# The last 64 features of the fp4 down product: split factors in rounded float32

## The chip, the cores and the metric

The kernel runs on one core of a Trainium2 chip. The metric is the device time of one execution in microseconds (us); the time before is the median of three runs, 2608.18 us (2606.8 to 2610.64). The engines are named TensorE (PE in the profile; its weight loads PEld), VectorE (DVE), ScalarE (ACT), GpSimd (POOL) and SyncE (SP, which issues most DMAs; SPq is its queue).

## The reference

The reference is a stack of six residual blocks on x of 8 x 1024 tokens with 256 features. The change concerns the first and the third block, which are the same feed-forward with fp4 quantization:

```python
def fp4_quant_dequant(x):              # blocks of 16 along the last dim
    scale = max(max(abs(xb)) / 6.0, 1e-12)
    idx = searchsorted(_MID, abs(xb / scale))
    return _GRID[idx] * sign(xb) * scale
...
gate = fp4_linear(x, w_gate)           # 256 -> 704
y = fp4_linear(x, w_up)                # 256 -> 704
h = silu(gate) * y
return fp4_linear(h, w_down)           # 704 -> 256, both sides quantized
...
x = x + 0.5 * _L0_ffn_ref(_layernorm(x), ...)
```

Between them lies a linear attention with decay, behind them a ternary feed-forward, an attention with memories, and the ternary feed-forward again.

## The kernel before

All of x stays on the chip as 16 groups X[g] of 4 tiles of 128 tokens, 64 tiles in all. `ffn_fp4` runs twice, once as the first stage (`prepare` true, when it also prepares weights for itself and later stages) and once as the third. It is one loop of steps: step i makes the hidden features of tile i and works off earlier tiles.

In step i TensorE makes the gate product pg and the up product pu for two halves of 352 features (L835, float32). ScalarE applies silu (L846), VectorE multiplies into h (L848). VectorE takes the blocks' maxima and their reciprocals (L783 to L787), and GpSimd divides h by its scales (L791). In step i+1 ScalarE writes the magnitudes into a PSUM area qp (L795) and VectorE rounds in two operations, the second into a bfloat16 grid gd (L858). gd has 768 columns for 704 features: the last 64 are filled with zeros once.

The grid is turned by DMA, not by TensorE. TensorE transposes only the scales (pts, L863), ScalarE copies them to sct (L869), and SP issues, in this order: sct to DRAM (sd, L871), the grid's DMA transpose gt (L884), and a load that spreads each scale over its 16 features (ht, L876, 384 KB). Two steps later GpSimd multiplies ht by gt (`scaled_turn`, L899). One step after that `down` makes the product po of six chunks of 128 features by wd (L932), and VectorE adds it to X (L941). The last chunk holds 64 features; its other rows are zeros in ht and in wd. The last two tiles take another way (`turn`): TensorE transposes h itself.

The normalized inputs go the same way, in halves of a group. Every odd step ScalarE normalizes two tiles (L317, L325, four operations) for a group two ahead; GpSimd divides them by their scales in the even step; in the next odd step ScalarE and VectorE round them to a grid gx in the same memory (mgx, L795 and L858). SP turns it in the even step after that (gtx, L1048), behind gt and ht. The next normalizing of that half overwrites the grid and so waits for gtx, and so does GpSimd's product xt (L899).

The order on each engine is written out by hand: `pin` ties every instruction to the one before it on its engine, so an engine that waits holds back everything behind it. `copies` is a list of ScalarE copies that are issued after the first silu of the next step. Weights for the down product are rounded and turned in steps 1 to 5 of the first stage (`prep_down_scale`, `prep_down`, `prep_down_turn`).

Of the kernel before, what the change touches and what calls it, by code (L numbers as in the profile page):

```python
# [9 lines left out]
F32 = mybir.dt.float32  # L10
F32R = mybir.dt.float32r
# [3 lines left out]
ALU = mybir.AluOpType  # L15
# [3 lines left out]
P = 128  # L19
D = 256  # L20
# [3 lines left out]
G = 4  # L24
# [15 lines left out]
def macaron_kernel(  # L40
# [25 lines left out]
    nc = tc.nc  # L66
    NB, S, _ = x.shape
# [3 lines left out]
    NI = w_gate.shape[0]  # L71
# [5 lines left out]
    DCH = [(k, min(P, NI - k)) for k in range(0, NI, P)]  # L77
    NC = len(DCH)
# [17 lines left out]
    w_f0 = f0_stack.enter_context(tc.tile_pool(name="w_f0", bufs=1))  # L96
# [43 lines left out]
    wd_n = raw.tile([P, 2, NI], F32, name="wd_n")  # L140
# [32 lines left out]
    ident = const.tile([P, P], F32, name="ident")  # L173
# [57 lines left out]
    pin, behind = order_keeper()  # L231
# [209 lines left out]
    def turned_part(xt, k):  # L441
        return xt.rearrange("p (j k) t -> p k j t", k=2)[:, k]

    wd = w_f0.tile([P, NC, D], F32, name="wd")
    nc.gpsimd.memset(wd[DCH[-1][1] :, NC - 1, :], 0.0)
    with (
        tc.tile_pool(name="prep_ps", bufs=2, space=PSUM, side="right") as prep_ps,
        tc.tile_pool(name="prep_pq", bufs=1, space=PSUM, side="right") as prep_pq,
# [160 lines left out]
        for k in range(2):  # L609
            pt = prep_ps.tile([P, TG], F32, tag="pt", name="pt")  # L610
# [22 lines left out]
    def prep_down(c):  # L633
        fp4_round(wd_n[:, c, :], wd_sc.pop(c), raw, nc.gpsimd, pin)

    def prep_down_turn(ps, tag):
        for i, (k0, kn) in enumerate(DCH):
            pt = ps.tile([P, D], F32, tag=tag, name="ptd")
            for c in range(2):
                pin(  # L640
                    nc.tensor.transpose(
                        pt[:kn, c * P : (c + 1) * P], wd_n[:, c, k0 : k0 + kn], ident
                    )
                )
            pin(nc.scalar.copy(wd[:kn, i, :], pt[:kn, :]))


    def load_a0():
# [96 lines left out]
    def ffn_fp4(prepare, after):  # L745
        with ExitStack() as st:
# [8 lines left out]
            xts, hs, hts = {}, {}, {}  # L755
# [1 line left out]


            gd = gp.tile([P, NC * P], BF16, name="gd")
            nc.gpsimd.memset(gd[:, NI:], 0.0)  # L760
            scales = []
            for n in range(2):
                sc = gp.tile([P, P], F32, name=f"sc_{n}")
# [12 lines left out]
            DOWN = 5  # L776
            HT_BUFS = DOWN if prepare else 4

            def scale(v, pool, at, mul=nc.gpsimd, sc=None):
                vb = v.rearrange("p (b k) -> p b k", k=16)  # L780
                _, nb, _ = vb.shape
                am, sp = qp[:, at : at + nb], qp[:, at + nb : at + 2 * nb]
                pin(nc.vector.tensor_reduce(am, vb, AX.X, ALU.max, apply_absolute_value=True))  # L783
                pin(nc.vector.tensor_scalar(sp, am, -1.0 / 6.0, -1e-12, ALU.mult, ALU.min))
                rs = pool.tile([P, nb], F32, tag="q_rs", name="q_rs")
                pin(nc.vector.tensor_scalar(rs, sp, -FP4_TIE, None, ALU.mult))
                pin(nc.vector.reciprocal(rs, rs))  # L787
                if sc is None:
                    sc = pool.tile([P, nb], F32, tag="q_sc", name="q_sc")
                copies.append(lambda: pin(nc.scalar.copy(sc, sp)))  # L790
                pin(mul.tensor_tensor(vb, vb, rs[:, :, None].to_broadcast([P, nb, 16]), ALU.mult))  # L791
                return sc

# [72 lines left out]
            def spread(i, pt):  # L866

                sct = hp.tile([P, P], F32, tag="sct", name="sct", bufs=1)
                pin(nc.scalar.copy(sct, pt))  # L869
                sd = dp.tile([8, 16, P], F32, tag="sd", name="sd")  # L870
                pin(nc.sync.dma_start(out=sd.rearrange("b c t -> c b t"), in_=sct))  # L871

                def wide(out, c0, c1):
                    part = sd[:, c0:c1, :].rearrange("b c t -> b (c t)")
                    pin(
                        nc.sync.dma_start(  # L876
                            out=out.rearrange("p c t -> p (c t)"),
                            in_=part[:, None, :].to_broadcast([8, 16, (c1 - c0) * P]),
                        )
                    )  # L880

                def turn_grid():
                    gt = hp.tile([P, NC, P], BF16, tag="gt", name="gt", bufs=2)
                    pin(nc.sync.dma_start_transpose(out=gt, in_=gd))  # L884
                    turning[i] = gt

                turn_grid()
                ht = hp.tile([P, NC, P], F32, tag="ht", name="ht", bufs=HT_BUFS)
                wide(ht, 0, NC)
                spreading[i] = ht  # L890
                if i in xhalf:
                    to, half = xhalf.pop(i)
                    if half == 0:
                        xts[to] = lnp.tile([P, 2 * G, P], F32, tag="xt", name="xt")
                    wide(xts[to][:, G * half : G * half + G, :], NC, NC + G)

            def multiplied(wide, grid):
# [4 lines left out]
                    )  # L902
                )

            def scaled_turn(i):
                hs.pop(i)
                ht = spreading.pop(i)
                multiplied(ht, turning.pop(i))
                hts[i] = (ht, P)

            def turn(i):
                h, _ = hs.pop(i)
                ht = hp.tile([P, NC, P], F32, tag="ht", name="ht", bufs=HT_BUFS)
                for c0, c1 in ((0, 4), (4, 5), (5, 6)):
                    kn = DCH[c0][1]
                    pa = ps_t.tile([P, 4, P], F32, tag="pt", name="pt")
                    for c in range(c0, c1):
                        k0 = DCH[c][0]
                        pin(
                            nc.tensor.transpose(pa[:kn, c - c0, :], h[:, k0 : k0 + kn], ident)  # L920
                        )
                    pin(nc.scalar.copy(ht[:kn, c0:c1, :], pa[:kn, : c1 - c0, :]))
                hts[i] = (ht, DCH[-1][1])

            def down(i, ps=ps_o, tag="po"):
                g, j = divmod(i, G)
                ht, tail = hts.pop(i)
                po = ps.tile([P, D], F32, tag=tag, name="po")
                for c in range(NC):
                    kn = tail if c == NC - 1 else P  # L930
                    pin(
                        nc.tensor.matmul(  # L932
                            po,
                            lhsT=ht[:kn, c, :],
                            rhs=wd[:kn, c, :],
                            start=(c == 0),
                            stop=(c == NC - 1),
                        )
                    )
                pin(  # L940
                    nc.vector.scalar_tensor_tensor(  # L941
                        X[g][:, j, :], po, 0.5, X[g][:, j, :], ALU.mult, ALU.add
                    )
                )
# [49 lines left out]
            for i in range(NT + 3):  # L994
# [82 lines left out]
                if i < NT:  # L1077
                    own = scales[i % 2] if by_dma(i) else None
                    if own is not None:
                        scale(h, hp, NI, sc=own[:, : NI // 16])  # L1080
                        hs[i] = (h, own)
                    else:
                        hs[i] = (h, scale(h, hp, NI) if i < NT - 1 else None)

                    if j % 2 == 0 and i > 1:
                        to_s, half_s = ((i + 6) // G, 0) if j == 2 else ((i + 4) // G, 1)
                        if 1 < to_s < NG:
                            scale(
                                x_part(half_s), lnp, NI + 88,
                                sc=own[:, NC * 8 : NC * 8 + 2 * D // 16],  # L1090
                            )
                            xhalf[i] = (to_s, half_s)
                    if j % 2 == 1 and i > 1:
                        to_r, half_r = ((i + 5) // G, 0) if j == 3 else ((i + 3) // G, 1)
                        if 1 < to_r < NG:
                            v = x_part(half_r)
                            mg = ps_t.tile([P, 2 * D], F32, tag="pt", name="mgx")
                            magnitudes(v, mg)
                            gx = v.bitcast(BF16)[:, 0 : 2 * D]
                            round_grid(v, mg, gx)  # L1100
                            xgrids[to_r, half_r] = (gx, i)
                    if i == 0:
                        nb = 2 * D // 16
                        for n in range(2):
                            round_(
                                v1[:, 2 * D * n : 2 * D * (n + 1)],
                                sc1[:, nb * n : nb * (n + 1)], mgs[n],
                            )
                    ln.advance(i, 0)
                    if NT - 18 <= i < NT - 2:  # L1110
                        begin(after, NT - 2 - i)
                if prepare and i == DOWN:
                    prep_down_turn(ps_t, "pt")
                if i >= DOWN or not prepare:
                    first = downs
                    while downs <= (i - 4 if i < NT else i - 3) and downs < first + 2:
# [968 lines left out]
```

## Time and profile before

| what | value |
|---|---|
| median of three runs | 2608.18 us |
| the profiled execution | 2604.35 us |
| its span, first to last instruction | 2602.6 us |
| PE busy | 2504.2 us, 96% |
| DVE busy | 2107.9 us, 81% |
| ACT busy | 1235.8 us, 47% |
| POOL busy | 902.6 us, 35% |
| mean granted TensorE clock | 0.994 |

The span is what lies between the first and the last instruction on the slowest core; what the execution takes beyond it (1.75 us) lies outside. Busy shares are averages over six stages with different limits, so a stage's own windows tell more. A group of instructions is shown as line, engine, operation, output<-inputs, shapes, count, then total busy time and the mean of one in ns, then the idle time of the engine ahead of it and what ended it. A float32 matmul appears as two rows. The mean of one matmul includes its way through the array; how fast they follow one another is read from the chain or the timeline. In the timeline a row begins with its start and its length, both in us.

### The profile page before, as it was taken

How to read it: one execution, taken by the hardware profiler on the slowest of the kernel's cores; microseconds unless marked ns; L12 is line 12 of the kernel's file. 1: busy time of each engine (PE TensorE's matmuls, PEld its weight loads, DVE VectorE, ACT ScalarE, POOL GpSimd, SP SyncE). 2: the span in 40 equal slices, each digit the busy share in tenths (PEclk: the TensorE clock that was granted, in tenths of full speed). 3: DMA queues.
4: the chain of work that ended last, by engine and by line, in shares of the span. 5: the costliest groups of instructions: out<-in, count | busy, mean ns of one | idle time of the engine just before them, and what ended most of it. 6: DMA issues, size and time to landing. Idle time of an engine off the chain costs nothing.

```text
span 2602.6 us, 52695 instructions
## 1 busy us (share of the span) xinstructions
PE 2504.2 (96%) x20426; PEld 1864.2 (72%) x20426; DVE 2107.9 (81%) x5040; ACT 1235.8 (47%) x2785; POOL 902.6 (35%) x895
## 2 busy tenths in 40 slices
PE   4899999999999998999999999999999999999999
PEld 2566776766666665677777789995677767678998
DVE  7899999858777678998889789657888888879864
ACT  5344444433433333444444366665555555437664
POOL 4555555521100102555555400004555555540000
PEclk9899999999999999999999999999999999999999
DMA  7455565510000001556555300000000000000001
GB/s 218 99 111 120 119 114 112 110 32 2 2 2 2 2 2 29 113 117 116 115 114 118 81 1 1 1 1 1 2 2 2 2 2 2 2 2 25 33 33 42
DMA packets 197883, 130.32 MB, mean 50 GB/s; under 512 B 137824, under 2 KB 173696, under 8 KB 197632
## 3 DMA queue, kind: packets, MB, share of 16 engines
q1 hardware_dynamic: 196688, 125.75, 22.3%
q8 instruction: 161, 2.64, 0.4%
q0 software_dynamic: 240, 0.54, 0.1%
q14 instruction: 90, 0.74, 0.1%
q10 hardware_dynamic: 704, 0.66, 0.1%
HBM read 78.67 MB, written 16.52 MB: 37 GB/s over the span
## 4 chain that ended last, share of the span: by engine, by line
PE 80%; DVE 11%; ACT 3%; DMA 3%; issue 2%; POOL 1%; SPq 1%; DVEq 0%; POOLq 0%; ACTq 0%
PE po L932 10%; PE po L1207 9%; PE pg L835 9%; PE ph L1180 9%; PE pu L835 8%; PE sc L1250 5%; PE py L1334 5%; PE pq L1348 4%; PE pkv L1348 4%; PE pk L1348 4%; PE po L1348 4%; PE py L1316 2%; PE pmo L1765 2%; DVE at L1259 1%; DMA gtx<-xn 1%
## 5 line engine op out<-in xcount | busy, mean ns | idle before, releaser
L835 PE MATMUL pg<-wgu,xt 128*128 128x352 f32 x1024 | 350.0, 465 | 13.4 <-ACT sg L846 13.1
L932 PE MATMUL po<-wd,ht 128*128 128x256 f32 x1536 | 356.0, 382 | 2.3 <-DVE x L941 1.8
L835 PE MATMUL pu<-wgu,xt 128*128 128x352 f32 x1024 | 348.9, 464 | 2.1 <-DVE h L848 1.9
L932 PEld LDWEIGHTS po<-wd,ht 128*128 128x128 f32 x1536 | 291.7, 191 | 66.0 <-issue 4.1
L791 POOL TENSOR_TENSOR h<-h,q_rs 128x704 f32<-128x704 f32 (+1 forms) x128 | 176.3, 1378 | 419.9 <-DVE q_rs L787 419.9
L846 ACT ACTIVATE sg<-pg 128x352 f32<-128x352 f32 x256 | 117.8, 460 | 399.3 <-PE pg L835 394.0
L835 PEld LDWEIGHTS pg<-wgu,xt 128*128 128x128 f32 x1024 | 194.9, 192 | 108.5 <-ACT sg L846 21.1
L835 PEld LDWEIGHTS pu<-wgu,xt 128*128 128x128 f32 x1024 | 187.1, 193 | 103.3 <-issue 14.7
L1207 PE MATMUL po<-w,hl 128*128 128x256 f32 x1024 | 243.9, 280 | 1.4 <-DVE hl L1191 1.2
L1207 PE MATMUL po<-w,hh 128*128 128x256 f32 x1024 | 243.4, 280 | 0.0
L1881 POOL TENSOR_TENSOR mo<-mo 128x256 f32<-128x256 f32 x192 | 164.3, 856 | 195.0 <-DVE mo L1778 186.5
L899 POOL TENSOR_TENSOR ht<-gt,ht 128x768 f32<-128x768 bf16 x124 | 206.4, 1664 | 0.0
L1180 PE MATMUL ph<-xh,w 128*128 128x512 f32 x512 | 204.4, 401 | 1.4 <-ACT hf L1188 0.6
L1180 PE MATMUL ph<-xl,w 128*128 128x512 f32 x512 | 202.2, 396 | 0.0
L1191 DVE TENSOR_TENSOR hl<-hf,hh 128x512 fp32r<-128x512 f32 x256 | 168.2, 683 | 39.6 <-ACT hh L1189 36.1
L1207 PEld LDWEIGHTS po<-w,hl 128*128 128x128 f32 x1024 | 192.1, 188 | 4.5 <-DVE hl L1191 2.5
L1207 PEld LDWEIGHTS po<-w,hh 128*128 128x128 f32 x1024 | 192.0, 188 | 2.6 <-DVE x L1215 0.3
L848 DVE TENSOR_TENSOR h<-sg,pu 128x352 f32<-128x352 f32 x256 | 131.6, 514 | 60.0 <-PE pu L835 53.1
L1188 ACT ACTIVATE hf<-ph,b1c 128x512 f32<-128x512 f32 x256 | 168.3, 696 | 18.5 <-PE ph L1180 16.1
L1259 DVE TENSOR_TENSOR at<-sc,dec 128x512 f32<-128x512 f32 x256 | 158.5, 681 | 16.6 <-PE sc L1250 16.5
L1259 DVE TENSOR_TENSOR at<-sc,tri 128x512 f32<-128x512 f32 x256 | 164.6, 678 | 0.4 <-PE sc L1250 0.4
L1189 ACT CAST hh<-hf 128x512 fp32r<-128x512 f32 x256 | 149.2, 628 | 17.0 <-PE po L1207 15.2
(276 smaller groups left out, 5304.0 us busy)
## 6 DMA issues: line engine op xcount, KB each, us to landing
ht<-sd SPq DMA_DIRECT2D x124, 384.0 KB
xt<-sd SPq DMA_DIRECT2D x56, 256.0 KB
sd<-sct SPq DMA_DIRECT2D x124, 64.0 KB
x<-in_x SPq DMA_DIRECT2D x15, 512.0 KB
out<-x SPq DMA_DIRECT2D x15, 512.0 KB
raw_w<-in_w_t SPq DMA_DIRECT2D x2, 1024.0 KB
gt<-gd SPq DMA_TRANSPOSE x124
gtx<-xn SPq DMA_TRANSPOSE x56
```

The source lines that it names most:

```text
L791: pin(mul.tensor_tensor(vb, vb, rs[:, :, None].to_broadcast([P, nb, 16]), ALU.mult))
L835: nc.tensor.matmul(ps, lhsT=xts[g][:, 2 * j + k, :], rhs=wgu[:, k, (2 * q + of_up) * NHALF : (2 * q + of_up + 1) * NHALF], start=(k == 0), ...
L899: nc.gpsimd.tensor_tensor(wide.rearrange("p c t -> p (c t)"), grid.rearrange("p c t -> p (c t)"), wide.rearrange("p c t -> p (c t)"), ALU. ...
L932: nc.tensor.matmul(po, lhsT=ht[:kn, c, :], rhs=wd[:kn, c, :], start=(c == 0), stop=(c == NC - 1),)
L1180: nc.tensor.matmul(ph, lhsT=w1[:, k, f * P : (f + 1) * P], rhs=xt[:, k, :], start=(k == 0 and xt is xh), stop=(k == 1 and xt is xl),)
L1188: nc.scalar.activation(hf, ph, AF.Gelu, bias=b1c[:, f : f + 1])
L1189: nc.scalar.copy(hh[:, f, :], hf)
L1191: nc.vector.tensor_tensor(hl[:, f, :], hf, hh[:, f, :].bitcast(F32), ALU.subtract)
L1207: nc.tensor.matmul(po, lhsT=ht[:, f, j * P : (j + 1) * P], rhs=w2[:, f, :], start=(f == 0 and ht is hh), stop=(f == NF - 1 and ht is hl),)
L1259: nc.vector.tensor_tensor(at, sc.rearrange("p m (e t) -> p (m e) t", e=2), weight, ALU.mult)
L1348: nc.tensor.matmul(dst, lhsT=lhsT, rhs=rhs, start=n == 0, stop=n == len(parts) - 1)
L1881: summed = nc.gpsimd.tensor_tensor(mo[:, :, :, 0, :], mo[:, :, :, 0, :], mo[:, :, :, m, :], ALU.add)
```

## The change

The last 64 features of the down product fill the whole array. Their rows stand twice in both factors: in gd the last 64 columns are copied behind themselves, and so are the last four scales, so ht's last chunk holds the 64 features twice. The weight tile ws holds, for the same 64 features, the rounded high part (float32r) in its first 64 rows and the remainder in its last 64. ht's last chunk is split for every tile into hh, its rounding to float32r (ScalarE), and hl, the remainder (GpSimd). The last float32 matmul of `down` becomes two float32r matmuls, hh by ws and hl by ws, whose sum is (high + remainder) x (high + remainder).

The fills with zeros go. `prep_down_turn` makes ws through a spare tile; `turn` doubles the last 64 features on GpSimd before its transposes, and moves its transposes into two groups of three.

```diff
-    wd = w_f0.tile([P, NC, D], F32, name="wd")
-    nc.gpsimd.memset(wd[DCH[-1][1] :, NC - 1, :], 0.0)
+    NK = DCH[-1][1]
+    wd = w_f0.tile([P, NC - 1, D], F32, name="wd")
+    ws = w_f0.tile([P, D], F32R, name="ws")
...
-    def prep_down_turn(ps, tag):
+    def prep_down_turn(ps, tag, pool):
+        spare = pool.tile([P, G, D], F32, tag="xn1", name="wt", bufs=1)
+        wt = spare[:, 0, :].rearrange("p (c n k) -> p c n k", c=2, n=2)
+        for c in range(2):
+            pin(nc.gpsimd.tensor_copy(
+                    wt[:, c], wd_n[:, c, None, NI - NK :].to_broadcast([P, 2, NK])))
...
+                wh = spare[:, 1, :].bitcast(F32R)
+                pin(nc.scalar.copy(wh, pt))
+                pin(nc.scalar.copy(ws[:NK], pt[:NK]))
+                pin(nc.vector.tensor_tensor(
+                        ws[NK:], pt[NK:], wh[NK:].bitcast(F32), ALU.subtract))
...
-            nc.gpsimd.memset(gd[:, NI:], 0.0)
...
-                copies.append(lambda: pin(nc.scalar.copy(sc, sp)))
+                copies.append(lambda: pin(nc.scalar.copy(sc[:, :nb], sp)))
+                if tail:
+                    copies.append(
+                        lambda: pin(nc.scalar.copy(sc[:, nb : nb + tail], sp[:, nb - tail :])))
...
+                pin(nc.scalar.copy(gd[:, NI:], gd[:, NI - NK : NI]))
                 turn_grid()
...
+            def split(ht):
+                hh = hp.tile([P, P], F32R, tag="hh", name="hh", bufs=3 if prepare else 2)
+                pin(nc.scalar.copy(hh, ht[:, NC - 1, :]))
+                hl = hp.tile([P, P], F32R, tag="hl", name="hl", bufs=3 if prepare else 2)
+                pin(nc.gpsimd.tensor_tensor(
+                        hl, ht[:, NC - 1, :], hh.bitcast(F32), ALU.subtract))
+                return hh, hl
+
             def scaled_turn(i):
                 hs.pop(i)
                 ht = spreading.pop(i)
                 multiplied(ht, turning.pop(i))
-                hts[i] = (ht, P)
+                hts[i] = (ht, *split(ht))
...
             def turn(i):
...
+                hd = lnp.tile([P, G, D], F32, tag="xn1", name="hd", bufs=1)[:, 0, 0:P]
+                pin(nc.gpsimd.tensor_copy(hd[:, 0:NK], h[:, NI - NK :]))
+                pin(nc.gpsimd.tensor_copy(hd[:, NK:], h[:, NI - NK :]))
-                for c0, c1 in ((0, 4), (4, 5), (5, 6)):
+                for c0, c1 in ((0, 3), (3, NC)):
...
             def down(i, ps=ps_o, tag="po"):
...
-                for c in range(NC):
-                    kn = tail if c == NC - 1 else P
+                factors = [(ht[:, c, :], wd[:, c, :]) for c in range(NC - 1)]
+                factors += [(hh, ws), (hl, ws)]
+                for n, (left, right) in enumerate(factors):
...
-                        scale(h, hp, NI, sc=own[:, : NI // 16])
+                        scale(h, hp, NI, sc=own, tail=NK // 16)
```

More of the change, by code (lines that the diff above doesn't have):

```diff
@@ L634, in prep_down @@
         fp4_round(wd_n[:, c, :], wd_sc.pop(c), raw, nc.gpsimd, pin)
-    def prep_down_turn(ps, tag):
-        for i, (k0, kn) in enumerate(DCH):
+    def prep_down_turn(ps, tag, pool):
+        spare = pool.tile([P, G, D], F32, tag="xn1", name="wt", bufs=1)
+        wt = spare[:, 0, :].rearrange("p (c n k) -> p c n k", c=2, n=2)
+        for c in range(2):
+            pin(
+                nc.gpsimd.tensor_copy(
+                    wt[:, c], wd_n[:, c, None, NI - NK :].to_broadcast([P, 2, NK])
+                )
+            )
+        for i, (k0, _) in enumerate(DCH):
             pt = ps.tile([P, D], F32, tag=tag, name="ptd")
             for c in range(2):
-                pin(
-                    nc.tensor.transpose(
-                        pt[:kn, c * P : (c + 1) * P], wd_n[:, c, k0 : k0 + kn], ident
+                if i < NC - 1:
+                    part = wd_n[:, c, k0 : k0 + P]
+                else:
+                    part = wt[:, c].rearrange("p n k -> p (n k)")
+                pin(nc.tensor.transpose(pt[:, c * P : (c + 1) * P], part, ident))
+            if i < NC - 1:
+                pin(nc.scalar.copy(wd[:, i, :], pt))
+            else:
+                wh = spare[:, 1, :].bitcast(F32R)
+                pin(nc.scalar.copy(wh, pt))
+                pin(nc.scalar.copy(ws[:NK], pt[:NK]))
+                pin(
+                    nc.vector.tensor_tensor(
+                        ws[NK:], pt[NK:], wh[NK:].bitcast(F32), ALU.subtract
                     )
                 )
-            pin(nc.scalar.copy(wd[:kn, i, :], pt[:kn, :]))
     def load_a0():
@@ L777, in ffn_fp4, with scale @@
             HT_BUFS = DOWN if prepare else 4
-            def scale(v, pool, at, mul=nc.gpsimd, sc=None):
+            def scale(v, pool, at, mul=nc.gpsimd, sc=None, tail=0):
                 vb = v.rearrange("p (b k) -> p b k", k=16)
@@ L789, in scale @@
                     sc = pool.tile([P, nb], F32, tag="q_sc", name="q_sc")
-                copies.append(lambda: pin(nc.scalar.copy(sc, sp)))
+                copies.append(lambda: pin(nc.scalar.copy(sc[:, :nb], sp)))
+                if tail:
+                    copies.append(
+                        lambda: pin(nc.scalar.copy(sc[:, nb : nb + tail], sp[:, nb - tail :]))
+                    )
                 pin(mul.tensor_tensor(vb, vb, rs[:, :, None].to_broadcast([P, nb, 16]), ALU.mult))
@@ L903, in multiplied @@
                 )
+            def split(ht):
+                hh = hp.tile([P, P], F32R, tag="hh", name="hh", bufs=3 if prepare else 2)
+                pin(nc.scalar.copy(hh, ht[:, NC - 1, :]))
+                hl = hp.tile([P, P], F32R, tag="hl", name="hl", bufs=3 if prepare else 2)
+                pin(
+                    nc.gpsimd.tensor_tensor(
+                        hl, ht[:, NC - 1, :], hh.bitcast(F32), ALU.subtract
+                    )
+                )
+                return hh, hl
             def scaled_turn(i):
@@ L913, in turn @@
                 ht = hp.tile([P, NC, P], F32, tag="ht", name="ht", bufs=HT_BUFS)
-                for c0, c1 in ((0, 4), (4, 5), (5, 6)):
-                    kn = DCH[c0][1]
-                    pa = ps_t.tile([P, 4, P], F32, tag="pt", name="pt")
-                    for c in range(c0, c1):
[L918 to L923, printed above, removed]
+                hd = lnp.tile([P, G, D], F32, tag="xn1", name="hd", bufs=1)[:, 0, 0:P]
+                pin(nc.gpsimd.tensor_copy(hd[:, 0:NK], h[:, NI - NK :]))
+                pin(nc.gpsimd.tensor_copy(hd[:, NK:], h[:, NI - NK :]))
+                for c0, c1 in ((0, 3), (3, NC)):
+                    pa = ps_t.tile([P, 3, P], F32, tag="pt", name="pt")
+                    for c in range(c0, c1):
+                        part = h[:, c * P : (c + 1) * P] if c < NC - 1 else hd
+                        pin(nc.tensor.transpose(pa[:, c - c0, :], part, ident))
+                    pin(nc.scalar.copy(ht[:, c0:c1, :], pa[:, : c1 - c0, :]))
+                hts[i] = (ht, *split(ht))
             def down(i, ps=ps_o, tag="po"):
                 g, j = divmod(i, G)
-                ht, tail = hts.pop(i)
+                ht, hh, hl = hts.pop(i)
                 po = ps.tile([P, D], F32, tag=tag, name="po")
-                for c in range(NC):
-                    kn = tail if c == NC - 1 else P
+                factors = [(ht[:, c, :], wd[:, c, :]) for c in range(NC - 1)]
+                factors += [(hh, ws), (hl, ws)]
+                for n, (left, right) in enumerate(factors):
                     pin(
                         nc.tensor.matmul(
[L933 to L937, printed above, removed]
+                            po, lhsT=left, rhs=right, start=(n == 0), stop=(n == NC)
                         )
@@ L1112, in ffn_fp4 @@
                 if prepare and i == DOWN:
-                    prep_down_turn(ps_t, "pt")
+                    prep_down_turn(ps_t, "pt", lnp)
                 if i >= DOWN or not prepare:
```

## The prediction

> **What bounds the kernel now.** First the page: its span, the chain of work that ended last, and the group that the edit rewrites.
>
> ```profile
> span 2602.6 us, 52695 instructions
> ...
> PE 80%; DVE 11%; ACT 3%; DMA 3%; issue 2%; POOL 1%; SPq 1%; DVEq 0%; POOLq 0%; ACTq 0%
> ...
> L932 PE MATMUL po<-wd,ht 128*128 128x256 f32 x1536 | 356.0, 382 | 2.3 <-DVE x L941 1.8
> ```
>
> TensorE is 80% of the chain. The down product has 1536 rows for 2 stages x 64 tiles x 6 chunks = 768 float32 matmuls, so each is two passes. I then asked for busy time in the second fp4 stage's steady part.
>
> ```profile
> 1104.80:1476.70 371.90, 371.90 (x1451) 268.95 (x1451) 324.90 (x720) 155.78 (x392) 202.39 (x147) 1.00 0.56 114
> ```
>
> TensorE (second number) is busy in all 371.90 us at full granted clock, VectorE in 324.90 (87%), ScalarE 155.78, GpSimd 202.39. So a step (one 128-token tile) is as long as TensorE's work in it. The chain in order of time prices a pass; its columns are start, length, work.
>
> ```profile
> 1104.78 2.59 PE po L932 x12
> ...
> 1535.32 3.77 PE po L1207 x32
> ```
>
> Twelve float32 passes take 2.59 us (0.216 each); 32 passes of rounded float32 (float32r), same shape, take 3.77 (0.118 each). Last, the timeline of two steps (start, length, engine, line, work, then idle time before it and its releaser), from which every link below is read.
>
> ```profile
> 1312.98 2.75 PE L932 MATMUL po<-wd,ht 128*128 128x256 f32 x12
> ...
> 1313.21 1.24 SPq L884 DMA_TRANSPOSE gt<-gd  x1
> ...
> 1314.59 0.60 SPq L876 DMA_DIRECT2D ht<-sd  x1
> ...
> 1315.24 1.20 SPq L1048 DMA_TRANSPOSE gtx<-xn  x1
> ...
> 1317.69 0.76 ACT L795 ACTIVATE qp<-h 128x704 f32<-128x704 f32 x1
> ...
> 1318.21 1.66 POOL L899 TENSOR_TENSOR ht<-gt,ht 128x768 f32<-128x768 bf16 x1
> ...
> 1319.57 0.89 DVE L858 SCALAR_TENSOR_TENSOR gd<-qp,h 128x704 bf16<-128x704 f32 x1
> ...
> 1319.69 0.26 ACT L869 COPY sct<-pts 128x128 f32<-128x128 f32 x1
> ...
> 1320.18 0.51 ACT L317 ACTIVATE xn<-x,ln_b 128x256 f32<-128x256 f32 x1 [0.23 <-DMA gtx<-xn]
> ...
> 1320.32 1.16 POOL L899 TENSOR_TENSOR xt<-gtx,xt 128x512 f32<-128x512 bf16 x1 [0.44 <-DMA gtx<-xn]
> ...
> 1320.42 2.75 PE L932 MATMUL po<-wd,ht 128*128 128x256 f32 x12
> ...
> 1322.08 0.58 ACT L795 ACTIVATE mgx<-xn 128x512 f32<-128x512 f32 x1
> ...
> 1323.23 1.39 POOL L791 TENSOR_TENSOR h<-h,q_rs 128x704 f32<-128x704 f32 x1 [1.75 <-DVE q_rs L787]
> ...
> 1324.39 0.46 ACT L846 ACTIVATE sg<-pg 128x352 f32<-128x352 f32 x1 [1.74 <-PE pg L835]
> ...
> 1325.04 0.76 ACT L795 ACTIVATE qp<-h 128x704 f32<-128x704 f32 x1
> ...
> 1326.09 0.88 DVE L858 SCALAR_TENSOR_TENSOR h<-qp,h 128x704 f32<-128x704 f32 x1
> ...
> 1327.00 0.89 DVE L858 SCALAR_TENSOR_TENSOR gd<-qp,h 128x704 bf16<-128x704 f32 x1
> ...
> 1328.09 1.24 SPq L884 DMA_TRANSPOSE gt<-gd  x1
> ```
>
> Step length: product to product, 1320.42 - 1312.98 = 7.44 us, two steps 14.87. Steps alternate. An odd one (the one of 1320) normalizes two tiles on ScalarE (1320.18 to 1322.08), and that waits for the turned x grid (gtx) that SP issued in the even step before; GpSimd multiplies xt with the same grid. In the present order GpSimd is free of ScalarE here: xt starts 0.14 us after the normalizing starts.
>
> **What it removes.** Per tile one float32 chunk, 2 x 0.216 = 0.432 us, becomes two float32r passes, 2 x 0.118 = 0.236: 0.196 us less, 25.1 us for 128 tiles. If float32r cost as much here as float32 passes the gain would be 0; if streaming alone counts, as in the hidden product's 32 passes of twice the width (7.47 us in the same chain, so 0.117 per 256 columns), it is the same 0.196. I take 0.196: a step could fall to 7.24, two to 14.48. Three fills with zeros go as well, ahead of everything that waits: 0.
>
> **What it adds to a step.** ScalarE: a 64-column copy inside gd (nearest row: L790, 44 columns, 0.19; I take 0.20), behind VectorE's gd and ahead of the grid's transpose on SP; a 4-column copy (at most that 0.19), off the path while the next ScalarE work waits for GpSimd; and hh, 128x128 (nearest row sct, 128x128, 0.26; bounds 0.19 and 0.35). GpSimd: hl, 128x128. By its two-input rows of 256 columns (731 ns, L1968) and 1024 (2374 ns, L1470), 2.14 ns a column, 0.46 us; bounds 0.40 and the nearest in width, 0.65 (L1659, 128 columns, another operation). TensorE uses hl in the next step, some 4 us later: no wait there. DMA sizes stay the same.
>
> **Where these stand is what matters.** In the odd step the built order is, on ScalarE: sct, gd's copy, four normalizing operations, hh, mgx, silu; on GpSimd: ht, hl, xt, h. So hl waits for hh, hh stands behind the normalizing, and behind hl are queued xt and the product of h with its scales. For h waits ScalarE's magnitude (qp), for that VectorE's rounding, then gd's copy, SP's grid transpose, the wide ht load and, behind both, the gtx transpose, for which the next odd step's normalizing waits. That closes a ring over two steps which did not exist before. From normalizing to normalizing, by the rows:
> four operations 1.90; hh 0.26; hand-over 0.10; hl 0.46; xt 1.16; h 1.39; hand-over 0.10; qp 0.76; hand-over 0.10; two roundings 1.80 (1326.09 to 1327.89); hand-over 0.10; gd's copy 0.20; to SP 0.20 (1327.89 to 1328.09); gt to gtx 2.03 (1313.21 to 1315.24); gtx issue to normalizing 4.94 (1315.24 to 1320.18). Sum 15.50; rows that follow one another on one engine overlap by 0.04 to 0.09, so I take off 0.16: 15.34 us.
> Hand-overs between ScalarE, VectorE and GpSimd are bounded by 0.02 (sct's end to SP) and 0.20 (gd's end to SP); VectorE to GpSimd shows 0.14 (1323.09 to 1323.23). With the bounds of all unknowns the ring is 15.0 to 15.8.
> A second ring needs no DMA: the same to the end of the odd step's gd (8.03), then VectorE's gate, reduction and reciprocal of the even step (1313.02 to 1315.65: 2.63), 0.14, h 1.39, 0.10, qp 0.76, 0.10, roundings 1.80, 0.10, gd's copy 0.20, back to normalizing: 15.25 less the same overlaps, 15.1. So a shorter gtx transfer alone would not free it.
>
> 15.34 is 0.47 over today's two steps and 0.86 over what TensorE would need. TensorE runs ahead for a few steps (its next pg waits for a silu that has about 3 us to spare) and then stalls on ScalarE's silu, which stands behind qp.
>
> The Trainium skill's page "DMA: Bandwidth & Descriptors", section "Anatomy of one DMA — SWDGE (gpsimd) path", speaks against this ring. It gives a DMA about 2.0 us plus bytes over 436 GB/s, fitted for another issuing path; gtx's 128 KB would be back in an estimated 2.3 us, the first ring would be 12.7 and would not bind. This trace has 4.94 for gtx behind a 384 KB ht load, so the row decides.
>
> **The sum.** xt is made 56 times, two for each two-step ring: 28 rings a stage, 56 in all. 56 x 0.47 = +26.3. Outside the rings some five steps at each stage's end gain 0.196: -2.0. The weights' preparation (one step of the first stage) gets two GpSimd copies and a ScalarE copy more and one VectorE subtraction, in a step where TensorE already waits for such a copy: by a 128x256 copy of 0.37 and a VectorE operation of 0.42, with hand-overs, +1.0 to +2, I take 1.5; if hidden, 0. The last two tiles of a stage get GpSimd copies ahead of their transposes and hh, hl ahead of the product, 0.26 + 0.46 + 0.3 + hand-overs, less one eviction: about 1 each, half of it beside other work: +2 over four tiles (0 to 4). Total +27.8. On the profiled span 2602.6 this is 2630.4, on its execution (2604.35) 2632; the median of the three runs is 2608.18, 3.8 above that execution, so I forecast 2636.
>
> **Rivals.**
> Faster: the ring does not hold, and TensorE's saving arrives. It decides if two steps' ring is under 14.48, 0.86 under my sum. For it: TensorE busy all the time and the others at 87, 42 and 54%. Against: it needs twice the error that all unknown links hold together. 2608.2 - 25.1 + 3.5 = 2587.
> Tie: the ring is 14.7 to 15.0, where saving and stall nearly cancel: 56 x (-0.17 to 0.13) + 1.5 = 2600 to 2617; centre 2609. The slack of ScalarE (1.73 us ahead of silu at 1324.39) speaks for it, but that is the odd step's silu, not the link through GpSimd.
> Worse: in the first stage VectorE is at 65.2 of 70 us (200 to 270) with the ternary weights' work in it; if each stall there adds to VectorE's backlog, a ring costs 0.7 more: 2636 + 28 x 0.7 = 2656, and with the links at their upper bounds beyond 2670.
> The edit does not save: float32r passes beside float32 ones take 0.216. The ring binds all the same, so still 2636; only the faster rival falls, to 2612.
>
> **How the numbers follow.** Forecast 0.66 (2617 to 2655), worse 0.10 (to 2680), tie 0.09, faster 0.15. Leaving out most of the faster case and the far end of the worse one, the range is 2602 to 2666; the forecast's own is 2617 to 2655. About 0.2% (5 us) is what a measurement can tell from no change: below 2603 lie the faster case and a sliver of the tie, 0.16; within 2603 to 2613 most of the tie, 0.07; above, 0.77.
>
> **What would show it.** Right: steps of about 7.67 us while x grids are made and 7.24 after them; hl on GpSimd idle before it, released by ScalarE's hh, in odd steps; xt starting some 2.6 us after the normalizing instead of 0.14; h and qp over 1 us later; TensorE idle on silu. The product's ten float32 passes and two float32r ones at about 2.40 us would confirm the saving even so. Wrong: steps of 7.24 throughout with hl's wait in the shade of GpSimd's idle time; or steps well over 7.9 in the second stage, which would mean a link that I have not priced.

## The result, and the profile after

The changed kernel takes 2646.22 us, median of four runs (2644.22 to 2646.7), beside 2607.49 us of the kernel before in the same comparison: a ratio of 1.0143, with a 95% interval of 1.0128 to 1.0158. The forecast was 2636. The profiled execution's span went from 2602.6 to 2643.9 us.

First the page of the changed kernel: its span, the shares of the chain that ended last, the gate product and the new remainder.

```profile
span 2643.9 us, 53170 instructions
...
PE 58%; DVE 17%; issue 10%; POOL 9%; ACT 4%; DMA 1%; SPq 0%; POOLq 0%; ACTq 0%; DVEq 0%
...
L858 PE MATMUL pg<-wgu,xt 128*128 128x352 f32 x1024 | 356.2, 471 | 42.3 <-ACT sg L869 41.6
...
L935 POOL TENSOR_TENSOR hl<-ht,hh 128x128 fp32r<-128x128 f32 x128 | 58.4, 456 | 321.3 <-ACT hh L932 320.5
```

TensorE is on 58% of the chain where it was on 80%; VectorE rose from 11 to 17%, GpSimd from 1 to 9%, and "issue", time for which the profile shows no wait, from 2 to 10%. The gate product now waits 41.6 us for silu in all (13.1 before). The last line shows the new wait: GpSimd makes hl in 456 ns, yet it stood idle for 320.5 us ahead of it, until ScalarE had made hh. Not all of this idle time is a cost, as an experiment below shows; what counts is what stands behind it.

The timeline of the third stage shows the two steps that answer to those of the prediction (start, length, engine, line, work, idle time before it and its releaser).

```profile
1316.82 1.21 SPq L1081 DMA_TRANSPOSE gtx<-xn  x1
...
1322.00 0.51 ACT L317 ACTIVATE xn<-x,ln_b 128x256 f32<-128x256 f32 x1 [0.56 <-DMA gtx<-xn]
...
1323.89 0.28 ACT L932 CAST hh<-ht 128x128 fp32r<-128x128 f32 x1
...
1324.25 0.46 POOL L935 TENSOR_TENSOR hl<-ht,hh 128x128 fp32r<-128x128 f32 x1 [3.30 <-ACT hh L932]
...
1324.66 1.16 POOL L923 TENSOR_TENSOR xt<-gtx,xt 128x512 f32<-128x512 bf16 x1
...
1325.10 1.45 PE L858 MATMUL pg<-wgu,xt 128*128 128x352 f32 x4 [0.58 <-ACT sg L869]
1325.78 1.39 POOL L814 TENSOR_TENSOR h<-h,q_rs 128x704 f32<-128x704 f32 x1
...
1327.20 0.76 ACT L818 ACTIVATE qp<-h 128x704 f32<-128x704 f32 x1 [2.00 <-POOL h L814]
...
1328.92 0.89 DVE L881 SCALAR_TENSOR_TENSOR gd<-qp,h 128x704 bf16<-128x704 f32 x1
...
1329.85 0.24 ACT L910 COPY gd<-gd 128x64 bf16<-128x64 bf16 x1 [1.35 <-DVE gd L881]
...
1332.15 1.20 SPq L1081 DMA_TRANSPOSE gtx<-xn  x1
...
1337.02 0.51 ACT L317 ACTIVATE xn<-x,ln_b 128x256 f32<-128x256 f32 x1 [0.26 <-DMA gtx<-xn]
```

From gtx's issue at 1316.82 the normalizing waits until 1322.00; hh follows its four operations at 1323.89, then hl, xt, h, qp, gd, the copy inside gd, and, behind the grid's transpose and the ht load, gtx at 1332.15, for which the next normalizing waits until 1337.02. GpSimd's xt starts 2.66 us after the normalizing's start instead of 0.14. That is the ring, link by link. TensorE stood idle for 0.58 us ahead of pg at 1325.10, until silu was done.

The chain in order of time (start, length, work) says the same from the other side:

```profile
1309.34 1.17 POOL xt L923
...
1324.66 1.16 POOL xt L923
...
1339.69 1.16 POOL xt L923
```

xt follows xt after 15.32 and 15.03 us. Between them the chain has pieces of GpSimd, ScalarE and VectorE and none of TensorE. Ahead of each hl it has a piece of issue, 3.26 us from 1320.95 and 2.97 from 1336.27; the first is the time in which, by the timeline, hl waited 3.30 us for hh.

The length of steps is read from the starts of each step's first silu. Between the sixth and the 58th step a pair took 14.87 us in the median before, and 15.36 in the third stage and 15.32 in the first after the change. The span's 41.3 us come, but for rounding, from these places:

| place | predicted | measured |
|---|---|---|
| steps 6 to 58, first stage | +13.2 | +16.8 (400.1 to 416.9) |
| steps 6 to 58, third stage | +13.2 | +12.0 (388.3 to 400.3) |
| the stages' ends and what follows | +2 | +11.2 (4.2 and 7.0) |
| starts, last five steps | -0.5 | +1.2 |

The third row takes in the stages between and behind, which vary by themselves: in the kernel with TensorE's part alone (below), which has no split and no new copy, the same two places show -3.0 and +1.2.

### The profile page after: what moved, and what is told of

Its sections match the earlier page's. It is cut to its first block, busy times and chain, and to the rows that moved or that the text cites. A ratio compares the mean times of both kernels' runs of the same rounds, so it can differ in the third digit from the quotient of the medians.

```text
span 2643.9 us, 53170 instructions
## 1 busy us (share of the span) xinstructions
PE 2500.4 (95%) x20426; PEld 1843.4 (70%) x20426; DVE 2109.0 (80%) x5041; ACT 1289.7 (49%) x3158; POOL 959.8 (36%) x1030
## 4 chain that ended last, share of the span: by engine, by line
PE 58%; DVE 17%; issue 10%; POOL 9%; ACT 4%; DMA 1%; SPq 0%; POOLq 0%; ACTq 0%; DVEq 0%
PE po L1240 9%; PE ph L1213 8%; PE sc L1283 5%; PE py L1367 4%; POOL h L814 4%; PE pq L1381 4%; PE pkv L1381 4%; PE po L1381 4%; PE pk L1381 4%; POOL ht L923 3%; PE po L969 2%; PE py L1349 2%; DVE h L881 2%; DVE qp L802 2%; PE pg L858 2%
## 5 line engine op out<-in xcount | busy, mean ns | idle before, releaser
L858 PE MATMUL pg<-wgu,xt 128*128 128x352 f32 x1024 | 356.2, 471 | 42.3 <-ACT sg L869 41.6
L969 PE MATMUL po<-wd,ht 128*128 128x256 f32 x1280 | 304.4, 385 | 3.4 <-DVE x L974 3.4
L969 PEld LDWEIGHTS po<-wd,ht 128*128 128x128 f32 x1280 | 244.7, 193 | 62.2 <-POOL xn L814 8.9
L858 PEld LDWEIGHTS pg<-wgu,xt 128*128 128x128 f32 x1024 | 182.8, 192 | 149.0 <-ACT sg L869 76.7
L935 POOL TENSOR_TENSOR hl<-ht,hh 128x128 fp32r<-128x128 f32 x128 | 58.4, 456 | 321.3 <-ACT hh L932 320.5
L1503 POOL TENSOR_TENSOR x<-x,ob 128x1024 f32<-128x1024 f32 x16 | 37.7, 2357 | 335.0 <-ACT xn L317 335.0
```

Of the source, the lines that this page charges most:

```text
L858: nc.tensor.matmul(ps, lhsT=xts[g][:, 2 * j + k, :], rhs=wgu[:, k, (2 * q + of_up) * NHALF : (2 * q + of_up + 1) * NHALF], start=(k == 0), ...
L969: nc.tensor.matmul(po, lhsT=left, rhs=right, start=(n == 0), stop=(n == NC))
```

## The experiments

Times are medians beside the kernel before in the same comparison; ratios go with their 95% intervals. All edits are against the changed kernel, but for the first. The kernel before took 2605.99 to 2609.61 us in these comparisons, so a few us between runs of different comparisons say little.

**TensorE's part alone.**

```diff
...
-                for c in range(NC):
...
+                factors = [(ht[:, c, :], wd[:, c, :]) for c in range(NC - 1)]
+                factors += [(fixed, ws), (fixed, ws)]
```

> The kernel before, with only TensorE's part of the change: the last chunk of the down product becomes two float32r matmuls on two fixed tiles; the last 64 features' contribution is left out, and no copy, split or doubling is added per tile. Theory (TensorE bounds the steps, a float32r pass is 0.098 us shorter): steps fall from 7.44 to 7.24 us and the time by 128 x 0.196 = 25 us, to 2580 to 2590. Rival (beside float32 passes a float32r pass costs as much as they do): steps stay at 7.44, 2607.

Measured: 2591.22 us beside 2605.99, 0.9936 (0.9921 to 0.995). Steps did fall to 7.24 us, so a float32r pass among float32 ones is as cheap as the ternary stage said. But the gain is 15 us where 25 were expected: in steps 6 to 58 the third stage gained 7.7 us and the first only 1.3 (400.1 to 398.8). The windows of this kernel (from:to, length, then busy time of TensorE, its weight loads, VectorE, ScalarE and GpSimd, each with its count) suggest why.

```profile
200.00:270.00 70.00, 65.68 (x253) 45.94 (x252) 64.34 (x135) 27.55 (x70) 38.00 (x31) 0.98 0.63 122
1130.00:1460.00 330.00, 329.43 (x1320) 238.09 (x1319) 292.84 (x649) 142.54 (x358) 184.95 (x135) 1.00 0.58 117
```

In a window of the first stage VectorE is busy in 64.34 of 70 us (65.20 before) and TensorE in 65.68: VectorE's work is packed there. In the third stage TensorE is busy in 329.43 of 330. The chain of the kernel before agrees: from 1130 to 1480 it lies on TensorE alone, but from 130 to 540 the three products have 60% of it, VectorE 17% and the DMA of gtx 7%. That the shorter product counts for less there because of this is argued and not tested.

**The ring without TensorE's saving.**

```diff
-                factors += [(hh, ws), (hl, ws)]
+                factors += [(ht[:, NC - 1, :], ws.bitcast(F32))]
...
```

> The changed kernel with all its copies and splits, but the last chunk is again one float32 matmul (doubled features by both halves of the weights); hh and hl are made and not read. Theory (the ring through hh, hl, xt and h sets the steps, TensorE only waits): the time stays near that of the changed kernel, 2644 to 2652, pairs of steps near 15.4 us, and TensorE's wait for silu shrinks. Rival (the added work's cost and TensorE's saving add up): 25 us more, about 2671.

Measured: 2647.56 us, 1.0152 (1.0136 to 1.0167), which is the changed kernel's time. TensorE's saving is worth nothing while the ring stands. Its waits in the same stretch of the third stage (us in total, times, longest), first of the changed kernel, then of this one:

```profile
PE pg L858 <- ACT sg L869: 10.4, 20, 1.3
```

```profile
PE pg L858 <- ACT sg L869: 2.7, 5, 1.1
```

The longer product filled time that TensorE spent waiting.

**The same work without the wait.**

```diff
-                        hl, ht[:, NC - 1, :], hh.bitcast(F32), ALU.subtract
+                        hl, ht[:, NC - 1, :], ident, ALU.subtract
```

> The changed kernel with hl = last chunk minus a constant tile, so that GpSimd does the same operation in the same place but does not wait for ScalarE's hh; the true remainder of the features is left out. Theory (the wait of hl for hh behind the normalizing closes the ring): pairs of steps fall from 15.4 to about 14.5 us, 2588 to 2600. Rival (the added operations' own time on GpSimd and ScalarE costs it, not the wait): no change, 2646; a part of it between.

**hh ahead of the normalizing.**

```diff
+                if by_dma(i - 3):
+                    scaled_turn(i - 3)
                 if to_do and j % 2 == 1:
                     if j == 1:
...
-                if by_dma(i - 3):
-                    scaled_turn(i - 3)
```

> The changed kernel with the multiplication of ht and its split issued ahead of the normalizing in the step, so that ScalarE makes hh before its four normalizing operations; every instruction is kept. Theory (position behind the normalizing): GpSimd's xt and h no longer follow the normalizing, the ring is some 13.4 us and does not bind, 2588 to 2600. Rival (hl's wait for hh costs wherever hh stands, or the gd copy is what makes the grids late): 2635 to 2646.

Measured: 2619.01 us without the wait, 1.0044 (1.003 to 1.0059), and 2617.17 with hh early, 1.0035 (1.0022 to 1.0048). They take 27 and 29 us off, and in both the median pair of the third stage is back at TensorE's pace, 14.49 and 14.48. So it is the wait, and the wait's place behind the normalizing, that closed the ring; the added operations' own time did not. With hh early the timeline reads:

```profile
1343.90 0.29 ACT L932 CAST hh<-ht 128x128 fp32r<-128x128 f32 x1
...
1344.10 0.50 ACT L317 ACTIVATE xn<-x,ln_b 128x256 f32<-128x256 f32 x1
1344.27 0.46 POOL L935 TENSOR_TENSOR hl<-ht,hh 128x128 fp32r<-128x128 f32 x1 [1.01 <-ACT hh L932]
...
1344.68 1.16 POOL L923 TENSOR_TENSOR xt<-gtx,xt 128x512 f32<-128x512 bf16 x1
...
1346.42 1.39 POOL L814 TENSOR_TENSOR h<-h,q_rs 128x704 f32<-128x704 f32 x1 [0.57 <-DVE q_rs L806]
```

hh (1343.90) now stands ahead of the normalizing (1344.10), hl and xt follow at once, and h waits only for VectorE's reciprocal, 1.74 us after xt's start. GpSimd still stands idle ahead of hl, 83.7 us between 1130 and 1500 (118.6 in the changed kernel), and the steps are at TensorE's pace all the same: the idle time as such is not the cost, but what waits behind it. The expected 2588 to 2600 were missed by 19 and 17 us: they assumed TensorE's full 25 us, and did not allow for the loss at the stages' ends.

**The copy inside gd.**

```diff
+            nc.gpsimd.memset(gd[:, NI:], 0.0)
...
-                pin(nc.scalar.copy(gd[:, NI:], gd[:, NI - NK : NI]))
```

> The changed kernel without ScalarE's copy inside gd (the last 64 columns are zeros again); the product of the features with the remainder of the weights is left out. Theory: the copy is one link of the ring, 0.24 us and a hand-over of 0.1, so a pair of steps loses about 0.34 and the time 56 x 0.34 = 19 us: 2622 to 2632. Rival (the copy, by making every grid's transpose later, is the cause of the whole loss): 2590 to 2600.

Measured: 2629.86 us, 1.0086 (1.0069 to 1.0102), 16 us less than the changed kernel; the mean pair of the third stage fell from 15.40 to 15.00. The copy is one link of the ring, priced nearly right, and not its cause.

**hl at the end of the step.**

```diff
                 multiplied(ht, turning.pop(i))
-                hts[i] = (ht, *split(ht))
+                hts[i] = ht
...
+                if by_dma(i - 3):
+                    hts[i - 3] = (hts[i - 3], *split(hts[i - 3]))
                 if prepare and i == DOWN:
```

> The changed kernel with hh and hl issued at the end of the step, hl behind xt and h on GpSimd, hh behind mgx on ScalarE; every instruction is kept. Theory (what is queued behind hl makes the loss): xt and h no longer wait for the normalizing, 2588 to 2602, though hh still stands behind the normalizing. Rival (hh's place on ScalarE, ahead of silu, costs it): 2630 to 2646.

Measured: 2612.52 us, 1.0014 (1.0005 to 1.0023). Here hh stays behind the normalizing, but GpSimd comes to hl only after xt and h, when hh is mostly made: between 1130 and 1500 it waits 4.9 us for it in all, where it waited 118.6. Nothing is queued behind hl that the ring needs. This opens the ring at another link, and 34 us go.

**The ends of the stages.** In the changed kernel the third stage ends like this:

```profile
1528.65 0.30 ACT L932 CAST hh<-ht 128x128 fp32r<-128x128 f32 x1 [3.29 <-POOL ht L923]
...
1529.03 0.45 POOL L935 TENSOR_TENSOR hl<-ht,hh 128x128 fp32r<-128x128 f32 x1 [0.41 <-ACT hh L932]
...
1529.60 0.24 POOL L952 COPY hd<-h 128x64 f32<-128x64 f32 x1
...
1529.89 0.47 PE L957 MATMUL pt<-ident,hd 128*128 128x128 f32 x1 [6.83 <-POOL hd L952]
```

GpSimd makes hl, behind it the two copies that double the last features (hd), and only then can TensorE transpose them; in TensorE's queue all products of the last tiles stand behind this transpose, and it was idle for 6.83 us. The first stage ends with the same wait, 6.8 us. In the kernel before the products of the last tiles waited 0.20 us at this place:

```profile
1489.89 5.45 PE L932 MATMUL po<-wd,ht 128*128 128x256 f32 x24 [0.20 <-POOL ht L899]
```

```diff
+                if i == NT:
+                    turn(NT - 2)
...
+                        if q == 0:
+                            scaled_turn(i - 3)
...
-                if by_dma(i - 3):
+                if by_dma(i - 3) and i != NT - 1:
                     scaled_turn(i - 3)
-                if NT - 2 <= i - 2 < NT:
+                if i - 2 == NT - 1:
```

> The changed kernel with the order of the last two steps of each fp4 stage altered: the second last tile is turned ahead of the last split, and the split of the tile before is issued before the last tile's rounding. Theory (the stages' ends cost 11 us more than before, since TensorE waits 6.8 us for the doubling copies, which stand on GpSimd behind two splits): 4 to 10 us less, 2636 to 2642. Rival (that wait hides nothing that would come earlier): 2646.

Measured: 2637.87 us, 1.0115 (1.01 to 1.013), 8 us less. The copies now come first, the transpose does not wait, and one wait of 2.59 us for ht remains:

```profile
1518.98 0.33 PE L957 MATMUL pt<-ident,hd 128*128 128x128 f32 x1
...
1524.30 3.43 PE L969 MATMUL po<-wd,ht 128*128 128x256 f32 x10 [2.59 <-POOL ht L923]
```

**Both, and four that build on them.** First the two edits for hh early and for the ends together.

> Both orders together: hh ahead of the normalizing, and the altered ends of the stages; every instruction is kept. Theory: the two losses are apart and add up, so this is 4 to 10 us under the kernel with hh early alone, about 2586, and 20 us under the kernel before the change. Rival: 2630 to 2640, if the ring has another closing link.

Measured: 2607.95 us, 1.0003 (0.9993 to 1.0013): 9 us under hh early alone, so the losses add up as thought, but the sum is level with the kernel before, not 20 us under it. The 2586 goes with the 2588 to 2600 that were expected of hh early; 4 to 10 us under the measured 2617 is 2607 to 2613.

Then the two edits for hl late and for the ends.

> The changed kernel with hh and hl at the end of the step and the altered ends of the stages; every instruction is kept. Theory (the ring and the stages' ends are separate losses): the ends took 10 us off the changed kernel and the one with hh early, so this is 7 to 10 us under hl late alone, 2600 to 2605, some 5 us under the kernel before the change. Rival (the ends' gain is already had once hl stands late): 2612.

Measured: 2602.7 us beside 2608.79, 0.9978 (0.9969 to 0.9987). This one, hh and hl late and the ends reordered, beats both kernels, the one before by 6 us. TensorE's part alone was worth 15, so the added work still costs some 9 in this order; in steps 6 to 58 it is 5.1 us in the first stage (403.9 beside 398.8) and 1.9 in the third.

hh early, hl late, and the ends:

```diff
+                return hh, lambda: rest(ht, hh)
+
+            def rest(ht, hh):
                 hl = hp.tile([P, P], F32R, tag="hl", name="hl", bufs=3 if prepare else 2)
...
+                if by_dma(i - 3):
+                    ht, hh, hl = hts[i - 3]
+                    hts[i - 3] = (ht, hh, hl())
                 if prepare and i == DOWN:
```

> As the last, but ScalarE makes hh ahead of its four normalizing operations and only hl stands at the end of the step. Theory (hh right ahead of silu still holds TensorE up where VectorE lags): 2 to 4 us better than with hh at the step's end, 2597 to 2602. Rival (hh ahead of the normalizing makes the x grids later and that costs as much): the same, 2600 to 2605.

Measured: 2609.19 us, 1.0005 (0.9997 to 1.0014). The theory fell: hh ahead of the normalizing is 6.5 us worse than hh right ahead of silu, whether hl stands late (2609.19) or early (2607.95, both orders together). The two profiled executions show 4.0 us of it: 1.4 in the third stage's steps 6 to 58, -0.9 in the first's, the rest in the starts and ends. Its cause stays open.

The same with the copy on GpSimd, `scaled_turn` issued ahead of `spread`:

```diff
-                pin(nc.scalar.copy(gd[:, NI:], gd[:, NI - NK : NI]))
+                pin(nc.gpsimd.tensor_copy(gd[:, NI:], gd[:, NI - NK : NI]))
```

> As the last, with the copy inside gd made by GpSimd, behind ht and ahead of xt, so that ScalarE waits for VectorE's gd no more. Theory (ScalarE waits 71.6 us for gd in the second stage of the changed kernel, and the normalizing stands behind that wait): where VectorE lags, steps shorten, 2590 to 2599. Rival (GpSimd then waits for gd instead, with xt and h behind it): the same or up to 10 us more.

Measured: 2616.08 us, 1.0034 (1.0021 to 1.0046): 7 us more than the last, the rival's case. In the first stage GpSimd now waits for VectorE's grid (us in total, times, longest), with xt and h behind it:

```profile
POOL gd L910 <- DVE gd L881: 22.7, 6, 10.2
```

Last the edit for hh early together with the float32 product.

> hh ahead of the normalizing, but the last chunk again one float32 matmul, hh and hl made and not read. Theory (with the ring gone TensorE bounds the steps again, so its saving counts): 12 to 16 us more than with hh early alone (2617), as much as TensorE's part alone saved, 2629 to 2633. Rival (TensorE's saving counts in no order of this kernel): no change, 2617.

Measured: 2628.2 us, 1.008 (1.0067 to 1.0094), 11 us more than hh early alone. With the ring open TensorE's saving counts again, in this order a little less than the 15 us that it was worth alone. In steps 6 to 58 it is the same as alone: 7.7 us in the third stage (391.8 to 384.1) and 1.4 in the first (7.7 and 1.3 alone).

## Why the prediction was right, and where it was not

The sign and the mechanism held. The ring was summed to 15.34 us; the third stage's median pair is 15.36. That the two agree to 0.02 us is partly luck: from one normalizing to the next it took 14.7 to 16.9 us between 1130 and 1460. Its links: hl 0.46 as priced (456 ns), hh 0.29 for 0.26, the copy inside gd 0.24 for 0.20, gtx to the normalizing 5.18 and 4.87 for 4.94. Taking the wait away, moving hh ahead, and moving hl back each opened the ring; shortening one link shortened it; changing TensorE's work did not. Which of the two rings binds is not shown. In the third stage (1130 to 1500) ten of the normalizing's starts waited for gtx, 8.9 us in all, 3.9 of them once at the stage's end; the others followed gd's copy within 0.15 us, as the second ring would have it. The copy's own waits for VectorE, 71.6 us in 47 times, do not decide it, for with hh early, where neither ring binds, they are still 53.2 us in 48. No run opens one ring and leaves the other.

The Trainium skill's page "DMA: Bandwidth & Descriptors", section "Anatomy of one DMA — SWDGE (gpsimd) path", would have had gtx back in an estimated 2.3 us; 5.18 and 4.87 were measured again, so the row was right to decide. Its fixed part of about 2.0 us does agree with the small copy of the scales (64 KB, issued from SP), whose landing releases the ht load: 2.05 us, from 1312.54 to 1314.59 in the trace before.

The term that was mis-sized most is the stages' ends: +2 was priced, by adding the durations of the new operations; +11.2 was measured. What was missed is the order: the doubling copies stand on GpSimd behind two multiplications of ht and two splits, and a split waits for ScalarE's hh; and TensorE's last products stand behind the transpose of those copies. Reordering them gave 8 us back. Beside this the rings' +28.8 us in steps 6 to 58 are close to the 26.3 forecast, so most of what the forecast of 2636 missed lies in this term.

The second is TensorE's saving. 25.1 us were put on 128 tiles at 0.196 us; alone it was worth 15, and in the first stage's steps 6 to 58 only 1.3. The forecast needed it only in the last steps, so it cost little there, but the faster rival at 2587 was never to be had: TensorE's part alone, with nothing added, took 2591. The change cost more in the first stage: 16.8 us over the 28 rings where 13.2 were summed, its mean pair 16.04 (15.39 before) beside a median of 15.32 (14.87). The rival that put 0.7 us a ring on VectorE's backlog there was too large, for the excess is 0.13; that it comes from the backlog is not shown, and with hh early, the ring open, these steps were still 3.5 us longer than before. The tie did not happen, and the rival of a float32r pass as dear as a float32 one fell with the first experiment.

## What to carry to other kernels

Before adding an operation to an engine with a hand-written order, list what is queued behind it and follow that work around until it comes back to the operation's own input; if it comes back, compare the sum of the ring with the steps it spans, whatever the engines' idle shares say. A wait for a small operation (here a copy of 0.29 us) can last as long as what stands ahead of that operation in its own queue. Look at the last iterations apart: the same new operations stand in another order there, and no steady state hides them.

## What the runs showed of the hardware that was not expected

A ScalarE copy of 4 columns took 170 ns in the mean, and one of 44 columns about 190: between these two sizes the time hardly depends on the size. The 124 copies of four scales cost ScalarE 21.1 us. Two float32r passes behind ten float32 ones of the same 256 columns did not slow each other: the product of 12 passes took 2.39 to 2.40 us, as the sum of 10 x 0.216 and 2 x 0.118 says.
